# A decoder layer on one Trainium2 core: row maxima scored in pairs of units between whole projection steps

## The chip, the cores and the metric

The kernel runs on one core of one Trainium2 chip. Its engines work side by side, each through its own list of instructions in order: PE (TensorE, the matmuls, with PEld for its weight loads), DVE (VectorE), ACT (ScalarE), POOL (GpSimd) and SP, which issues most of the transfers. They wait for each other by semaphores. Matmuls write to PSUM, which only PE, DVE and ACT reach; the kernel uses it as four tiles. The metric is the device time of one execution in microseconds (us), lower is better.

## The reference

One layer of a decoder in float32, for 4 batches of 512 rows and 512 columns: a causal self attention with 16 heads of 32 columns, a causal cross attention whose keys and values are the context itself (masked scores are -10000, not minus infinity), and a feed-forward part with a gate over 8 experts of which the two highest logits give the weight. Each part takes a layernorm of x and is added to x.

```python
def _layernorm(x, axis=-1, eps=1e-05):
    m = jnp.mean(x, axis=axis, keepdims=True)
    v = jnp.var(x, axis=axis, keepdims=True)
    return (x - m) / jnp.sqrt(v + eps)
...
    def _L0_attn_ref(x, q_w, q_b, k_w, k_b, v_w, v_b, o_w, o_b):
        B, T, H, NH = (4, 512, 512, 16)
        HD = H // NH
        SCALE = HD ** (-0.5)
...
        q = (x @ q_w.T + q_b).reshape(Bd, Td, NH, HD).transpose(0, 2, 1, 3)
        k = (x @ k_w.T + k_b).reshape(Bd, Td, NH, HD).transpose(0, 2, 1, 3)
        v = (x @ v_w.T + v_b).reshape(Bd, Td, NH, HD).transpose(0, 2, 1, 3)
        scores = jnp.einsum('bhqd,bhkd->bhqk', q, k) * SCALE
        causal = jnp.tril(jnp.ones((Td, Td), dtype=bool))
        scores = jnp.where(causal, scores, -jnp.inf)
        probs = jax.nn.softmax(scores, axis=-1)
        ctx = jnp.einsum('bhqk,bhkd->bhqd', probs, v)
        ctx = ctx.transpose(0, 2, 1, 3).reshape(Bd, Td, Hd)
        return ctx @ o_w.T + o_b
...
            scores = jnp.where(causal[None, None], scores, jnp.asarray(MASKED_BIAS, scores.dtype))
            attn = jax.nn.softmax(scores, axis=-1)
            out = jnp.einsum('bhqk,bhkd->bhqd', attn, vh)
...
        logits = jnp.einsum('bsd,ed->bse', x, W_gate)
        routing_weights, selected_experts = jax.lax.top_k(logits, TOP_K)
        shared_out = jnp.einsum('bsd,od->bso', jax.nn.relu(jnp.einsum('bsd,od->bso', x, W_up)), W_down)
        rw = jax.nn.softmax(routing_weights, axis=-1)
        expert_out = jnp.einsum('bsd,do->bso', x, W_expert)
        moe_out = jnp.sum(rw, axis=-1, keepdims=True) * expert_out
        return shared_out + moe_out
    x = x + _L0_attn_ref(_layernorm(x, axis=-1), L0_attn_q_w, ...)
    x = x + _L0_xattn_ref(_layernorm(x, axis=-1), ctx_2048, ctx_2048)
    x = x + _L0_ffn_ref(_layernorm(x, axis=-1), L0_ffn_W_up, ...)
    return x
```

## The kernel before

All work is fp32 in blocks of 128 partitions. x, the queries, keys, values and the intermediate of the feed-forward part of one batch are tiles of 128 x 4 x 512. A *projection step* makes one 128 x 512 block with four accumulating matmuls (`project`, L221, and `project_t`, L233; both are generators that stop after each matmul, so that other work can be put between them). The steps are `query` and `key` (L595, L599), `value` (L642), `up`, `down`, `expert` (L743, L796, L807). `share` and `gate` (L754, L769) are short steps that make the gate's logits; `gate`'s results go through DVE and one ACT exponential into the weights `rw`.

The order on PE, DVE, ACT and POOL is written out by hand: what the Python code issues first stands first in an engine's list. Tiles in PSUM come from one pool of four (`ps`, L63; `pair`, L65, is one tile of 128 x 2 x 512, two banks). A tile's first matmul waits until what was in that place has been read.

The attention needs each row's maximum before the exponentials. `Attention.maxima` (L269) scores one *unit*: heads in four row groups of 32 partitions that work at the same time (L286), into two PSUM tiles; ACT copies each tile to SBUF (L297, in one of six `pt` buffers), POOL masks the diagonal blocks (L305), and DVE takes the maxima (L317). The reductions are not issued at once: `maxima` returns them as a list of *jobs*. A stage has ten units over four groups of heads (g = 0 to 3). When a group's last maxima are there, `split` (L334) cuts them into three bf16 parts, and `rows` (L345) turns these round on PE (L349) and copies them to a row tile `mrow` (L355). `masked` (L359, cross only) broadcasts such a row by a matmul (L363) and takes an exponential (L365); the `weigh` that it returns multiplies the sums `beh` of later keys by it (L371 to L373, on DVE, or on POOL inside the stage).

`with_maxima` (L869) runs such a stage: after each unit it issues a share of the projection matmuls that are to fill PE, in proportion, wherever a step then stands, with one job of the unit before after each matmul. The rows of groups 0 and 1 are turned after units 5 and 7, those of group 2 at the end or, where there is little to fill with, in the attention. `late` tells the attention which rows are still to be made and at which of its units.

`attend` (L917) runs the attention itself in ten units: scores again, with the row maximum added by a bf16 matmul (`scores`, L377: L389, L400), the exponential on ACT (L423), the mask on POOL (L431), and, two units later, the product with the values (`shares`, L450: L462). Denominators come from summed blocks (L510 on DVE, L516 on PE) or from a second matmul with ones. In the cross attention, `divide` (L546: L550, L551 and `inverse`) needs the weighed sums of the group; `scale` (L529) ends a group.

The main loop (L963) runs for each batch b: `with_maxima` and `attend` for the self attention, the output projection, `with_maxima` and `attend` for the cross attention, then `add_cross` (L713: sixteen PE transposes, L718, added to x) and the layernorm and transposes for the feed-forward part (`norm_ffn`, L732). What fills the maxima stages: in batch 0, query, key and value of batch 0 (self) and query and key of batch 1 (cross); in batch 1, the gate, ups and downs of batch 0 (self) and query and key of batch 2 and the experts of batch 0 (cross); in batch 2, the gate, ups and downs of batch 1 (self) and query and key of batch 3 (cross); in batch 3, the experts of batch 1 (self) and the gate, ups and downs of batch 2 (cross). The values of the next batch stand around `add_cross`.

Two neighbouring blocks of a projection share one PSUM tile (`pm_qk`, `pm_v`, `pm_u`, `pm_d`, `pm_e`), and where it can be, one instruction takes both out (L647, L752, L805). `aside` (L823) takes two blocks of downs and two of experts out by ACT and adds them on POOL.

## Time and profile before

| | us |
|---|---|
| median of 3 runs | 811.29 (811.07 to 811.46) |
| the profiled execution, whole | 811.3 |
| the profiled execution, span of the trace | 809.6 |
| PE busy | 796.8 (98%) |
| DVE busy | 563.7 (70%) |
| ACT busy | 397.1 (49%) |
| POOL busy | 334.3 (41%) |

The span is the time from the first to the last instruction in the trace; 1.7 us lie around it. A timeline row gives the start, the time, the engine, the line, the operation with its output and inputs, the shapes, how many instructions were merged (x16), and in brackets how long the engine was idle before and what ended that. A 128x512 fp32 matmul stands in the trace as two rows. Busy times are shares of the whole span: a stage can have another limit.

### The profile page before, as it was taken

To read this page: it belongs to the slowest core of one execution; us is meant where nothing else is said; L and a number is where in the kernel's file an instruction comes from. 1 tells how busy PE (TensorE), PEld (TensorE's weight loads), DVE (VectorE), ACT (ScalarE), POOL (GpSimd) and SP (SyncE) were. 2 spreads that over 40 slices of the span, in tenths; PEclk is the share of its full clock that TensorE was granted. 3 is DMA by queue.
4 is the path that set the end of the run, shared out by engine and by line. 5 is a ranking of instruction groups with operands and counts; after the bars stand their busy time and mean duration, and the time that the engine had idled before them with its cause. 6 is when DMAs were issued, how large, how long until landed. Compare 5 with 4: busy or idle time off the path is not lost.

```text
span 809.6 us, 13953 instructions
## 1 busy us (share of the span) xinstructions
PE 796.8 (98%) x5616; PEld 379.0 (47%) x5616; DVE 563.7 (70%) x955; ACT 397.1 (49%) x450; POOL 334.3 (41%) x525
## 2 busy tenths in 40 slices
PE   8999999999999999999999999999999999999998
PEld 7444454434444454444544445444444344444544
DVE  2478865879678854587867776697879764888512
ACT  2457426861547515666144752686068614674110
POOL 4334612554234732266233481366335543465100
PEclk9999999999999999999999999999999999999999
DMA  9601000001000000020100000000102000000101
GB/s 334 237 28 28 1 1 1 2 2 53 1 27 27 2 1 0 2 101 5 53 14 14 1 2 1 0 2 2 53 28 70 10 1 0 1 2 2 52 1 52
DMA packets 13681, 24.51 MB, mean 30 GB/s; under 512 B 1968, under 2 KB 2224, under 8 KB 13616
## 3 DMA queue, kind: packets, MB, share of 16 engines
q1 hardware_dynamic: 13184, 22.96, 8.3%
q8 instruction: 44, 0.72, 0.4%
q10 hardware_dynamic: 432, 0.66, 0.2%
q14 instruction: 21, 0.17, 0.1%
HBM read 19.42 MB, written 4.19 MB: 29 GB/s over the span
## 4 chain that ended last, share of the span: by engine, by line
PE 86%; DVE 8%; ACT 3%; issue 1%; POOL 1%; DMA 0%
PE pm_qk L235 13%; PE pm_u L235 7%; PE pv_c L462 7%; PE pm_o L687 7%; PE pm_v L223 6%; PE pm_e L223 6%; PE pm_d L223 5%; PE pv_s L462 5%; PE sc_c L389 5%; PE sm_s L286 5%; PE sm_c L286 5%; PE sc_s L389 4%; DVE nm_s L317 3%; DVE nm_c L317 2%; ACT sum_s L423 1%; PE sc_s L400 1%
## 5 line engine op out<-in xcount | busy, mean ns | idle before, releaser
L317 DVE TENSOR_REDUCE nm_c<-s_c 128x2 f32<-128x1024 f32 (+3 forms) x128 | 96.0, 811 | 37.1 <-POOL s_c L305 37.1
L317 DVE TENSOR_REDUCE nm_s<-s_s 128x2 f32<-128x1024 f32 (+3 forms) x128 | 96.9, 811 | 35.2 <-POOL s_s L305 35.2
L297 ACT COPY s_s<-sm_s 128x1024 f32<-128x1024 f32 x80 | 77.1, 1015 | 64.4 <-PE sm_s L286 34.9
L297 ACT COPY s_c<-sm_c 128x1024 f32<-128x1024 f32 x80 | 77.1, 1015 | 39.4 <-PE sm_c L286 23.0
L305 POOL TENSOR_SCALAR_AFFINE_SELECT s_c<-s_c 128x512 f32<-128x512 f32 (+1 forms) x80 | 43.9, 551 | 105.8 <-ACT s_c L297 105.8
L305 POOL TENSOR_SCALAR_AFFINE_SELECT s_s<-s_s 128x512 f32<-128x512 f32 (+1 forms) x80 | 43.8, 551 | 90.7 <-ACT s_s L297 90.7
L423 ACT ACTIVATE pt_c<-sc_c 128x1024 f32<-128x1024 f32 x64 | 61.7, 1031 | 20.5 <-PE sc_c L400 16.2
L510 DVE TENSOR_TENSOR sum_s<-sum_s,pt_s 128x256 f32<-128x256 f32 (+2 forms) x72 | 58.8, 882 | 14.9 <-PE pv_s L462 14.9
L431 POOL TENSOR_SCALAR_AFFINE_SELECT pt_c<-pt_c 128x512 f32<-128x512 f32 (+1 forms) x64 | 51.2, 808 | 26.4 <-ACT pt_c L423 25.9
L223 PE MATMUL pm_d<-wdown_sb,hT 128*128 128x512 f32 x128 | 61.1, 608 | 0.0
L423 ACT ACTIVATE pt_s<-sc_s 128x1024 f32<-128x1024 f32 x56 | 54.1, 1028 | 13.1 <-PE sc_s L400 7.0
L235 PE MATMUL pm_u<-fT,wup_sb 128*128 128x512 f32 x128 | 59.1, 604 | 0.0
L223 PE MATMUL pm_v<-wv_sb,xnT 128*128 128x512 f32 x128 | 58.8, 600 | 0.0
L687 PE MATMUL pm_o<-wo_sb,oT_s 128*128 128x512 f32 x128 | 57.8, 596 | 0.0
L235 PE MATMUL pm_qk<-xnT,wk_sb 128*128 128x512 f32 x120 | 57.3, 607 | 0.0
L223 PE MATMUL pm_e<-wexp_sb,fT 128*128 128x512 f32 x120 | 57.1, 606 | 0.0
L235 PE MATMUL pm_qk<-xnT,wq_sb 128*128 128x512 f32 x120 | 56.7, 604 | 0.0
L389 PE MATMUL sc_s<-qT,kT 32*128 32x128 f32 (+3 forms) x512 | 54.7, 463 | 1.5 <-ACT sum_s L423 1.1
L389 PE MATMUL sc_c<-cqT,ckT 32*128 32x128 f32 (+3 forms) x512 | 54.2, 462 | 0.9 <-ACT sum_c L423 0.9
L431 POOL TENSOR_SCALAR_AFFINE_SELECT pt_s<-pt_s 128x512 f32<-128x512 f32 (+1 forms) x56 | 47.3, 854 | 18.5 <-ACT pt_s L423 18.0
L286 PE MATMUL sm_s<-kT,qT 32*128 32x512 f32 (+3 forms) x512 | 47.5, 461 | 0.1
L286 PE MATMUL sm_c<-ckT,cqT 32*128 32x512 f32 (+3 forms) x512 | 46.1, 460 | 0.0
(166 smaller groups left out, 1274.0 us busy)
## 6 DMA issues: line engine op xcount, KB each, us to landing
cv<-in_ctx_dram SPq DMA_DIRECT2D x16, 256.0 KB, 3.9
out_dram<-x SPq DMA_DIRECT2D x15, 256.0 KB, 2.1
x<-in_x_dram SPq DMA_DIRECT2D x14, 256.0 KB, 4.1
xin<-in_x_dram SPq DMA_DIRECT2D x12, 256.0 KB, 2.6
wq_sb<-in_wq_dram SPq DMA_DIRECT2D x2, 512.0 KB, 6.3
wk_sb<-in_wk_dram SPq DMA_DIRECT2D x2, 512.0 KB, 7.9
wv_sb<-in_wv_dram SPq DMA_DIRECT2D x1, 1024.0 KB, 8.3
wo_sb<-in_wo_dram SPq DMA_DIRECT2D x1, 1024.0 KB, 9.8
```

The costliest lines, as they stand in the source:

```text
L223: nc.tensor.matmul(pm, lhsT=lhs_t[:, c, t * P : (t + 1) * P], rhs=w[:, c, :], start=(c == 0), stop=(c == NC - 1),)
L235: nc.tensor.matmul(pm, lhsT=w[:, c, f * P : (f + 1) * P], rhs=rhs_t[:, c, :], start=(c == 0), stop=(c == NC - 1),)
L286: nc.tensor.matmul(scs[r // 2][:, r % 2, c : c + (i + 1) * P], lhsT=self.q_t[h, g, i * P : (i + 1) * P], rhs=self.k_t[h, g, : (i + 1) * P] ...
L297: nc.scalar.copy(s, scs[n])
L305: nc.gpsimd.affine_select(out=diagonal, in_=diagonal, compare_op=ALU.is_ge, fill=NEG, base=0, pattern=[[0, 2], [0, len(pieces)], [-1, P]], ...
L317: nc.vector.tensor_reduce(self.nm[g][:, i, 2 * n : 2 * n + 2], made[n][:, :, c : c + (i + 1) * P], axis=AX.X, op=ALU.max, negate=True,)
L389: nc.tensor.matmul(scs[r // 2][:, r % 2, c : c + S - j * P], lhsT=self.k_t[h, g, j * P : (j + 1) * P], rhs=self.q_t[h, g, j * P :], start= ...
L423: nc.scalar.activation(pt, scs[n], AF.Exp)
L431: nc.gpsimd.affine_select(out=diagonal, in_=diagonal, compare_op=ALU.is_ge, fill=0.0, base=0, pattern=[[0, 2], [0, len(pieces)], [1, P]], ...
L462: nc.tensor.matmul(pv[r * HD : (r + 1) * HD, u, j * P :], lhsT=ones if u else self.v[:, j, h * HD : (h + 1) * HD], rhs=pts[r // 2][:, r % ...
L510: nc.vector.tensor_tensor(to, to, pts[n][:, :, c : c + S - j * P], ALU.add)
L687: nc.tensor.matmul(pms[t // 2][:, t % 2, :], lhsT=a.out[:, c, t * P : (t + 1) * P], rhs=wo_sb[:, c, :], start=(c == 0), stop=(c == NC - 1),)
```

## The change

A PSUM tile holds one block of a projection, in its first half, and each block is taken out by an instruction of its own: queries and keys at once by ACT, values by DVE, ups by ACT, downs by DVE (the last two of batch 2 by ACT and POOL), experts by DVE with the weight. `aside` is gone.

`with_maxima` scores two units directly after each other (ten units in five rounds) and then runs whole projection steps until half of the next step's matmuls would go beyond the share that is due. Jobs are the second unit's of the round before and the first unit's of this one. In a stage with steps to run beforehand (`first`, only batch 0) one step more is run beforehand. Counting rounds from 0, the rows of groups 0 and 1 are turned after the second matmul of rounds 2 and 3, `masked` comes after the third of rounds 3 and 4; the rows of group 2 are turned at the end only where the last round had two blocks, and otherwise in the attention at unit 3, with those of group 3 at unit 5. Where group 2 was turned in the stage, group 3 comes at unit 3, in the cross attention too. In the cross attention of a stage with a short last round, `masked` of groups 2 and 3 comes at units 6 and 7, and both are weighed at unit 9.

In the feed-forward lists, `gate` follows the first `up` where it followed the last; for batch 2, the first `up` moves from batch 3's cross to its self stage, and `gate` follows the third.

```diff
--- before.py
+++ after.py
@@ -593,23 +593,23 @@
         e.k_t = act.tile([P, NC, S], F32, tag="k_t", name=f"kT_{b}")
 
         def query(f):
-            made[f] = pair(f"pm_qk{b}_{f}")
-            yield from project_t(made[f][:, 0, :], wq_sb, e.xn_t, f)
+            out = pair(f"pm_q{b}_{f}")[:, 0, :]
+            yield from project_t(out, wq_sb, e.xn_t, f)
+            query_out(f, out)
 
         def key(f):
-            yield from project_t(made[f][:, 1, :], wk_sb, e.xn_t, f)
-            out(f)
-
-        def out(f):
+            out = pair(f"pm_k{b}_{f}")[:, 0, :]
+            yield from project_t(out, wk_sb, e.xn_t, f)
+            key_out(f, out)
+
+        def query_out(f, ps):
             nc.scalar.activation(
-                e.k_t[:, f, :], made[f][:, 1, :], AF.Identity, bias=bk_sb[:, f : f + 1]
-            )
+                e.q_t[:, f, :], ps, AF.Identity, bias=bqs_sb[:, f : f + 1], scale=SCALE
+            )
+
+        def key_out(f, ps):
             nc.scalar.activation(
-                e.q_t[:, f, :],
-                made[f][:, 0, :],
-                AF.Identity,
-                bias=bqs_sb[:, f : f + 1],
-                scale=SCALE,
+                e.k_t[:, f, :], ps, AF.Identity, bias=bk_sb[:, f : f + 1]
             )
 
         def half(n):
@@ -628,7 +628,8 @@
                         skip_group_check=True,
                     )
             if n == 1:
-                out(0)
+                key_out(0, made[0][:, 1, :])
+                query_out(0, made[0][:, 0, :])
 
         steps = [(lambda f=f, w=w: w(f)) for f in range(NC) for w in (query, key)]
         if b == 0:
@@ -636,20 +637,13 @@
         return steps
 
     def value(e):
-        b, made = e.b, {}
+        b = e.b
         e.v = act.tile([P, NT, D], F32, tag="v", name=f"v_{b}")
 
         def one(t):
-            if t % 2 == 0:
-                made[0] = pair(f"pm_v{b}_{t}")
-            yield from project(made[0][:, t % 2, :], e.xn_t, wv_sb, t)
-            if t % 2 == 1:
-                nc.vector.tensor_tensor(
-                    e.v[:, t - 1 : t + 1, :],
-                    made[0],
-                    bv_sb.unsqueeze(1).to_broadcast([P, 2, D]),
-                    ALU.add,
-                )
+            made = pair(f"pm_v{b}_{t}")[:, 0, :]
+            yield from project(made, e.xn_t, wv_sb, t)
+            nc.vector.tensor_tensor(e.v[:, t, :], made, bv_sb, ALU.add)
 
         return [(lambda t=t: one(t)) for t in range(NT)]
 
@@ -745,11 +739,9 @@
                 made["h"] = act.tile(
                     [P, NC, S], F32, tag="o_t" if b != B - 2 else "f_t", name=f"hT_{b}"
                 )
-            if f % 2 == 0:
-                made["u"] = pair(f"pm_u{b}_{f}")
-            yield from project_t(made["u"][:, f % 2, :], wup_sb, f_t, f)
-            if f % 2 == 1:
-                nc.scalar.activation(made["h"][:, f - 1 : f + 1, :], made["u"], AF.Relu)
+            u = pair(f"pm_u{b}_{f}")[:, 0, :]
+            yield from project_t(u, wup_sb, f_t, f)
+            nc.scalar.activation(made["h"][:, f, :], u, AF.Relu)
 
         def share():
 
@@ -794,39 +786,24 @@
             nc.vector.tensor_reduce(made["rw"], ew, axis=AX.X, op=ALU.add)
 
         def down(t):
-            if t % 2 == 0:
-                made["d"] = pair(f"pm_d{b}_{t}")
-            yield from project(made["d"][:, t % 2, :], made["h"], wdown_sb, t)
-            if t == NT - 1 and b == B - 2:
-                for n in range(2):
-                    aside(f"d{b}_{n}", t - 1 + n, made["d"][:, n, :], 1.0)
-            elif t % 2 == 1:
-                both = e.x[:, t - 1 : t + 1, :]
-                nc.vector.tensor_tensor(both, made["d"], both, ALU.add)
+            d = pair(f"pm_d{b}_{t}")[:, 0, :]
+            yield from project(d, made["h"], wdown_sb, t)
+            xt = e.x[:, t, :]
+            if t >= NT - 2 and b == B - 2:
+
+                some = work.tile([P, D], F32, tag="xn", name=f"some_{b}_{t}", bufs=4)
+                nc.scalar.copy(some, d)
+                nc.gpsimd.tensor_tensor(xt, xt, some, ALU.add)
+            else:
+                nc.vector.tensor_tensor(xt, d, xt, ALU.add)
 
         def expert(t):
             if b == B - 1 and t == NT - 1:
                 yield from expert_parts(t)
                 return
-            last = b == B - 1 and t == NT - 2
-            if t % 2 == 0:
-                made["e"] = pair(f"pm_e{b}_{t}")
-            yield from project(made["e"][:, t % 2, :], f_t, wexp_sb, t)
-            for n in (0,) if last else (0, 1) if t % 2 == 1 else ():
-                u = t - t % 2 + n
-                if t == NT - 1 and b == B - 3:
-                    aside(f"e{b}_{n}", u, made["e"][:, n, :], made["rw"][:, u : u + 1])
-                    nc.sync.dma_start(out=out[b, u * P : (u + 1) * P, :], in_=e.x[:, u, :])
-                else:
-                    weigh(u, made["e"][:, n, :], slice(0, D), nc.sync)
-
-        def aside(name, t, ps, scale):
-
-
-            some = work.tile([P, D], F32, tag="xn", name=f"some_{name}", bufs=4)
-            nc.scalar.mul(some, ps, scale)
-            xt = e.x[:, t, :]
-            nc.gpsimd.tensor_tensor(xt, xt, some, ALU.add)
+            made_e = pair(f"pm_e{b}_{t}")[:, 0, :]
+            yield from project(made_e, f_t, wexp_sb, t)
+            weigh(t, made_e, slice(0, D), nc.sync)
 
         def weigh(t, ps, cols, queue):
             xt = e.x[:, t, cols]
@@ -870,47 +847,50 @@
 
 
         norms = list(norms)
-        run(steps[:first])
-        fill = matmuls(steps[first:])
-        total = sum(1 if step.__name__ in ("share", "gate") else NC for step in steps[first:])
+
+        run(steps[: first + (first > 0)])
+        steps = steps[first + (first > 0) :]
+
+        def matmuls_of(step):
+            return 1 if step.__name__ in ("share", "gate") else NC
+
+        total = sum(map(matmuls_of, steps))
 
         units = []
         for g in range(0, NC, 2):
             units += [[(g, 1), (g + 1, 1)]]
             units += [u for k in (g, g + 1) for u in ([(k, 2), (k, 0)], [(k, NT - 1)])]
-
-        lead = 2 if first else 0
-        for _ in range(lead):
-            next(fill)
-        done, due, jobs, late = lead, float(lead), [], {5 if a.cross else 3: NC - 1}
-        todo = []
-        for n, pieces in enumerate(units):
-            new = a.maxima(pieces)
-            if todo:
-                todo.pop()(nc.gpsimd)
-            if norms and n % 2 == 0:
-                new.append(norms.pop(0))
-            due += (total - lead) / len(units)
-
-            count = round(due) - done
-            for k in range(count):
-                next(fill, None)
-                done += 1
-                if k == min(1, count - 1) and n in (5, 7):
-                    jobs = a.rows((n - 5) // 2) + jobs
-                if k == min(1, count - 1) and a.cross and n in (6, 8):
-                    todo.append(a.masked((n - 6) // 2))
-                if n == len(units) - 1 and k == count - (2 if count > 4 else 1):
-                    if total >= 2 * len(units):
-                        a.rows(2)[0](nc.scalar.copy)
-                    else:
-                        late = {3: 2, 5: NC - 1}
+        done, jobs, todo = 0, [], []
+        for n in range(0, len(units), 2):
+            jobs += a.maxima(units[n])
+            for weigh in todo:
+                weigh(nc.gpsimd)
+            todo = []
+            new = a.maxima(units[n + 1])
+            if norms:
+                jobs.append(norms.pop(0))
+            part, count = [], 0
+            while steps and done + matmuls_of(steps[0]) / 2 <= total * (n + 2) / len(units):
+                part.append(steps.pop(0))
+                count += matmuls_of(part[-1])
+                done += matmuls_of(part[-1])
+
+            for k, _ in enumerate(matmuls(part)):
+                if k == 1 and n in (4, 6):
+                    jobs = a.rows(n // 2 - 2) + jobs
+                if k == 2 and a.cross and n in (6, 8):
+                    todo.append(a.masked(n // 2 - 3))
                 run(jobs[:1])
                 jobs = jobs[1:]
             run(jobs)
             jobs = new
-        for _ in fill:
-            pass
+        for weigh in todo:
+            weigh(nc.gpsimd)
+        late = {3: NC - 1}
+        if count >= 2 * NC:
+            a.rows(2)[0](nc.scalar.copy)
+        else:
+            late = {3: 2, 5: NC - 1}
         run(jobs)
         return late
 
@@ -939,9 +919,9 @@
             if n in late:
                 for copy in a.rows(late[n]):
                     copy(nc.scalar.copy)
-            if a.cross and n in (5, 7):
-                todo.append(a.masked(n // 2))
-            if n in (6, 9) and todo:
+            if a.cross and n in ((5, 7) if len(late) == 1 else (6, 7)):
+                todo.append(a.masked(2 + n // 7))
+            while todo and (n == 9 or n == 6 and len(late) == 1):
                 todo.pop(0)()
             if len(waiting) > 2:
                 values()
@@ -999,13 +979,14 @@
                 pass
             gates, ups, downs, experts = ffn(e)
             if b + 3 < B:
-                between_self, between_cross = gates[:1] + ups + gates[1:] + downs, experts
+                between_self = gates[:1] + ups[:1] + gates[1:] + ups[1:] + downs
+                between_cross = experts
             elif b + 2 < B:
-                between_self, between_cross = gates[:1] + ups + gates[1:] + downs, []
-                ahead = experts
+                between_self = gates[:1] + ups[:1] + gates[1:] + ups[1:] + downs
+                between_cross, ahead = [], experts
             elif more:
-                between_self, ahead = ahead, experts
-                between_cross = gates[:1] + ups + gates[1:] + downs
+                between_self, ahead = ahead + ups[:1], experts
+                between_cross = gates[:1] + ups[1:3] + gates[1:] + ups[3:] + downs
             else:
                 run(gates[:1] + ups + gates[1:])
                 run(downs[:2] + experts[:2] + downs[2:] + experts[2:])
```

## The prediction

> **What bounds the kernel now.** I read the page's busy times first, then the chain of waits, then the timeline of single stages, engine by engine.
>
> ```profile
> PE 796.8 (98%) x5616; PEld 379.0 (47%) x5616; DVE 563.7 (70%) x955; ACT 397.1 (49%) x450; POOL 334.3 (41%) x525
> ...
> PE 86%; DVE 8%; ACT 3%; issue 1%; POOL 1%; DMA 0%
> ```
>
> The tensor engine (PE) is almost never without work, at a granted clock of 1.00 in every stretch I read, and 86% of the chain that ends last is its own. So what counts is how long PE needs for its list, and each wait that the change puts into that list. The change is made in the eight maxima stages (two for each batch: self and cross). This is the timeline of the cross stage of batch 0:
>
> ```profile
> 129.06 1.15 PE L286 MATMUL sm_c<-ckT,cqT 32*128 32x384 f32 x16
> 130.14 1.98 PE L235 MATMUL pm_qk<-xnT,wk_sb 128*128 128x512 f32 x4
> 130.30 1.93 ACT L297 COPY s_c<-sm_c 128x1024 f32<-128x1024 f32 x2 [1.07 <-PE sm_c L286]
> ...
> 132.06 1.14 PE L286 MATMUL sm_c<-ckT,cqT 32*128 32x512 f32 x8
> 132.16 0.69 ACT L604 ACTIVATE kT<-pm_qk,bk_sb 128x512 f32<-128x512 f32 x1
> ...
> 133.13 1.98 PE L235 MATMUL pm_qk<-xnT,wq_sb 128*128 128x512 f32 x4
> ```
>
> A unit starts every 2.99 us (129.06, 132.06, then 135.04). Two rows of the trace are one projection matmul; eight rows in a run take 3.43 us, so one takes 0.859 and two 1.72. A unit's own streaming is 0.86 (in the attention after it, sixteen such rows from 251.95 to 252.81, with row-tiled work on both sides). What is left, 2.99 - 1.72 - 0.86 = 0.41, is what going from full-array to row-tiled matmuls and back costs. The copies out of PSUM start 1.24 after the unit (130.30 - 129.06), and two take 1.93.
>
> **Part 1: two units together.** Each of 5 pairs in 8 stages saves one such round trip: 40 x 0.41 = 16.4 us. But PSUM has four tiles, a pair takes all four, and the order of the changed program shows every first projection after a pair waiting for the copy of the first unit's first tile. The attention loop has the same situation: a third unit meets four occupied tiles.
>
> ```profile
> 252.15 1.94 ACT L423 ACTIVATE sum_s<-sc_s 128x1024 f32<-128x1024 f32 x2 [0.69 <-PE sc_s L400]
> ...
> 253.23 0.30 PEld L389 LDWEIGHTS sc_s<-qT,kT 32*128 32x128 f32 x4 [0.22 <-ACT sum_s L423]
> ```
>
> The first exponential of 0.97 to 1.02 ends near 253.15, PE goes on 0.08 later. So after a pair: copy starts at 1.24, ends at 2.24, PE is released at 2.32, and with some 0.1 for a full weight load the projection starts 2.40 after the pair, where without the wait it would be 1.07 + 0.86 = 1.93. A pair then costs 2.40 + 0.19 (back to row-tiled: 1.91 for two matmuls of 1.72) = 2.59, against 2 x (2.99 - 1.72) = 2.54 now. The saving is used up: +0.05 x 40 = **+2.0 us**. Ends: released at 2.26 with nothing added, 40 x -0.09 = -3.6; started at 2.55, 40 x 0.20 = +8.
>
> The Trainium skill, TensorEngine Tiling (Array Packing), Key Properties, says that changing the tiling mode drains the engine, which speaks for the change; by that alone the time would be the 811.3 less the 16.4 above, 795. The same page under PSUM Bottleneck speaks against it: tiling makes the matmuls faster but not the evacuation, which can become the limit; no price is given there, and the rows above decide.
>
> **Part 2: one block to a PSUM tile.** Evacuations get shorter and more: adds of 128x1024 at 1.22 become two of 0.68, relus of 1.02 two of 0.69. ACT's extra 8 x 0.36 lies in its idle time (24 of 31 us busy in the busiest stage for its length); that cover gone, it would be 3 us. VectorE (DVE) is in order, and here it matters where it stands at a stage's end. Now, in batch 1's self stage (attention starts at 250.77):
>
> ```profile
> 248.13 1.27 DVE L317 TENSOR_REDUCE nm_s<-s_s 128x2 f32<-128x768 f32 x2
> 250.65 1.22 DVE L805 TENSOR_TENSOR x<-pm_d,x 128x1024 f32<-128x1024 f32 x1 [1.25 <-PE pm_d L223]
> 251.79 1.27 DVE L317 TENSOR_REDUCE nm_s<-s_s 128x2 f32<-128x768 f32 x2
> 252.98 0.54 DVE L206 TENSOR_SCALAR xn_a<-xin,mv_a,rs_a 128x512 f32<-128x512 f32 x1
> 253.43 2.34 DVE L317 TENSOR_REDUCE nm_s<-s_s 128x2 f32<-128x1024 f32 x2
> ```
>
> DVE is waiting for PE there, it is not late. In the changed order it is tied to PE by the add of down block 1, which ends with the round before the last. From the last round's start T it then has, from T + 0.2: add 0.66, two reduces 1.23, four 2.46, a norm 1.25, two reduces 2.35, the split 0.9, add (block 2) 0.66, four reduces 2.46, add (block 3) 0.66: done at T + 12.8. (Durations from this stage's rows; single adds from L702, 678 ns.) The second score unit of the attention takes over block 3's PSUM tile. PE gets there at T + 2.40 + 8 x 0.859 + 0.33 (transposes) + 0.1 + 1.18 (first unit, 250.77 to 251.95) = T + 10.9. A wait of 1.9, and the same in batch 2: **+3.8** (ends 0 and 6). Behind the blocked matmul stand all scores, and ACT's exponentials with them.
>
> **Part 3: whole steps, so DVE's tie to a block's end comes in every round.** Where DVE evacuates single blocks (values in batch 0's self stage, experts in batch 3's self stage, downs in batch 3's cross stage), the second pair's transposes (L349) come early. Tied at a round's start R: add 0.66 to 0.75, reduces 1.27 and 2.35, split 0.9 (cross 1.2), so the parts are there at R + 5.3 to 5.6; PE asks at R + 2.40 + 1.72 = R + 4.1. Waits of 1.2, 1.3 and 1.4; with 0.3, 0.2 and 0.6 for the lesser ones (a late add, the first transposes) **+1.5, +1.5, +2.0** (ends 0 and 8 together). In the stages between, where ACT evacuates, DVE isn't tied and I find nothing.
>
> **Part 4: an up step moved from batch 3's cross to its self stage.** 4 x 0.859 is paid in both places, 0 in sum. In the self attention there PE now waits 1.43 and 0.27 because DVE is late; with 3.4 us more cover that goes: **-1.7** (ends -1.7, 0). The gate's steps cost PE the same 0.92 wherever they stand; only its tile comes free sooner.
>
> **Part 5: cross transposes and weighing moved.** Where the last round has one block (cross of batches 0, 2, 3), rows of group 2 go into the attention, and the weighing of group 2 goes from unit 6 to unit 9, in front of group 3's on DVE:
>
> ```profile
> 173.64 0.06 DVE L371 MEMSET ct_c<- 128x1 f32 x1 [1.37 <-ACT ct_c L365]
> 173.73 1.06 DVE L372 TENSOR_TENSOR behT<-ct_c,behT 128x512 f32<-128x512 f32 x1
> 174.83 0.69 DVE L373 TENSOR_TENSOR ct_c<-ct_c,cnt 128x512 f32<-128x512 f32 x1
> ...
> 185.61 0.06 DVE L371 MEMSET ct_c<- 128x1 f32 x1
> ...
> 188.17 0.69 DVE L550 TENSOR_TENSOR ct_c<-pv_c,ct_c 128x512 f32<-128x512 f32 x1 [0.43 <-PE pv_c L516]
> ...
> 193.97 0.69 DVE L532 TENSOR_TENSOR behT<-behT,dt_c 128x512 f32<-128x512 f32 x1
> ```
>
> At 173.64 the weighing is between two waits, free. After the other at 185.61 there is only 0.43 of slack, so 1.9 of weighing makes everything behind it 1.5 late, up to L532. The last four of the sixteen L718 transposes (PE from 193.30, twelve take 1.3) read that result: no slack. 3 x 1.5, and 0.2 each for the value evacuation now in front of the layernorm transposes: **+5.1** (ends 0, 6). Against it, unit 5 now has the L363 matmul right behind the transposes, and PE waits 2.3 us there over all (the L363 group's idle time, released by ACT); taken apart, **-2.3** (ends -2.3, 0).
>
> **Sum.** 2.0 + 3.8 + 1.5 + 1.5 + 2.0 - 1.7 + 5.1 - 2.3 = +11.9 on the span of 809.6, so 821.5; the profiled execution's 811.3 has 1.7 around the span, which gives 823.2, and the median of the runs (811.29) is the same as the profiled one. Forecast: **823 us**. No DMA is added or moved to another queue; POOL's adds for two expert blocks become DVE's (in part 3).
>
> **Rivals.** (a) Heavy: DVE's ties bite in every round, not only at these places. Then the pair's last score tile waits for a DVE add that stands behind a reduce of 1.21: 0.7 more in each of the 16 or so rounds that end with such a block, +11, to 834. For it: 563.7 us of in-order DVE work; against: ACT evacuates the other rounds, and the add's own end (0.15 + 0.66) lies just before the need at 0.95. (b) Wash: the copy's wait eats the switches, but DVE runs far enough ahead at the stages' ends and the tails have slack that I don't see: 809.6 + 2.0 - 1.7 - 2.3 + some 2 of ties, 811 to 812. Against it stands the missing slack at 193.97. (c) Faster, decided by one thing, the time from a pair's start to its first projection: if it is 2.26 instead of 2.40, pairs give -3.6, and if DVE's delays also stay hidden, the freed waits of 1.7 and 2.3 come on top: 804. It turns faster when that time is below 2.35 and the other terms are near nothing. Against it: the copy alone ends at 2.24. That the edit doesn't do what it says is excluded by the order of the instructions.
>
> **How the numbers follow.** Forecast 0.62, (a) 0.15, (b) 0.11, (c) 0.12. The forecast's own range is 816 to 830. Leaving out most of (c) and half of (a), the range is 809 to 833; the sum of all lower ends would be 804, of all upper ends 839. A difference under 0.2% (1.6 us) can't be told from none. Faster: (c) and a little of (b), 0.13; same: half of (b), 0.05; slower 0.82.
>
> **What would show it.** In a maxima stage, projections should start 2.3 to 2.5 after the first L286 of a pair, with waits on L297's copy; if 1.93, part 1 is wrong by 19 us. Around the start of batch 1's and 2's self attention, a PE wait of about 2 on the down add; in three stages a wait before L349; at the end of three cross attentions, a wait of 1.5 inside the transposes of add_cross. DVE waiting for PE at those places instead would make the forecast wrong, toward 811.

## The result, and the profile after

The changed kernel takes 820.92 us (median of 4 runs, 820.8 to 821.1) beside 811.37 (4 runs, 811.07 to 811.46) for the kernel before, measured with it: ratio 1.0119, 95% interval 1.0106 to 1.0131. It is slower by 9.5. The profiled spans are 819.1 and 809.6.

The page of the kernel after, its busy times and its chain of waits by engine:

```profile
PE 785.8 (96%) x5616; PEld 380.3 (46%) x5616; DVE 565.0 (69%) x972; ACT 398.2 (49%) x456; POOL 327.7 (40%) x523
...
PE 39%; DVE 11%; ACT 3%; issue 2%; DVEq 0%; ACTq 0%
```

PE is busy 11.0 less than before: switches were saved. The span is 9.5 longer all the same, so PE now waits some 20 us more. The chain of waits could here be followed back only to 368 us, over 55% of the span; of these 55%, VectorE has 11, a fifth, where before it had 8 of 99. The same stage as in the prediction, batch 0's cross stage, in the timeline of after:

```profile
133.76 2.01 PE L286 MATMUL sm_c<-ckT,cqT 32*128 32x512 f32 x24
134.99 3.76 ACT L297 COPY s_c<-sm_c 128x1024 f32<-128x1024 f32 x4 [0.43 <-PE sm_c L286]
136.05 3.70 PE L235 MATMUL pm_q<-xnT,wq_sb 128*128 128x512 f32 x8 [0.29 <-ACT s_c L297]
```

The pair starts at 133.76, the first of four copies at 134.99, and the projection at 136.05, 0.29 late, released by the copy. The waits that the prediction placed on VectorE (DVE), in self stage 0, cross stage 3, self attention 1 and at the end of cross attention 0:

```profile
55.42 0.38 PE L349 MATMUL mt_s<-identb,parts 128*128 128x128 bf16 x4 [1.06 <-ACT s_s L297]
...
710.96 0.40 PE L349 MATMUL mt_c<-identb,parts 128*128 128x128 bf16 x4 [1.29 <-DVE parts L343]
...
256.06 1.15 PE L389 MATMUL sc_s<-qT,kT 32*128 32x128 f32 x16 [1.62 <-DVE x L798]
...
197.91 0.66 PE L712 MATMUL tp_x<-ident,behT 128*128 128x128 f32 x4 [0.90 <-DVE behT L532]
```

All four places wait. (The first row names ACT, whose copy was long done; the transposes read what DVE's split writes.) In before, the sixteen transposes of the last place ran through without a wait:

```profile
193.30 2.08 PE L718 MATMUL tp_x<-ident,behT 128*128 128x128 f32 x16
```

By the starts of the first score matmuls of each stage and attention, this is where the time went, after less before:

| | stage | attention | from there to the next stage |
|---|---|---|---|
| self 0, with the lead in | +0.39 | +1.36 | 0.00 |
| cross 0 | +0.20 | +0.29 | +1.00 |
| self 1 | -0.98 | +1.21 | 0.00 |
| cross 1 | +0.32 | -0.07 | +0.06 |
| self 2 | -0.98 | +1.20 | 0.00 |
| cross 2 | +0.21 | +0.29 | +0.95 |
| self 3, less the moved step's 3.43 | +1.34 | -2.09 | 0.00 |
| cross 3, with it; last column to the last expert block | +2.55 | +0.78 | +1.12 |

The maxima stages, where the switches are saved, gain 2.0 in two places and lose 5.0 in the others, +3.05 in sum. The attentions add 2.97 and what stands between them and the next stage 3.13; 0.3 more lies behind the last row.

### The profile page after: what moved, and what is told of

It reads as the page before. It is cut to its first block, busy times and chain, and to the rows that moved or that the text cites. A ratio compares the mean times of both kernels' runs of the same rounds, so it can differ in the third digit from the quotient of the medians.

```text
span 819.1 us, 13977 instructions
## 1 busy us (share of the span) xinstructions
PE 785.8 (96%) x5616; PEld 380.3 (46%) x5616; DVE 565.0 (69%) x972; ACT 398.2 (49%) x456; POOL 327.7 (40%) x523
## 4 chain that ended last, share of the span: by engine, by line
PE 39%; DVE 11%; ACT 3%; issue 2%; DVEq 0%; ACTq 0%
PE pm_u L235 5%; PE pm_e L223 4%; PE pm_o L681 3%; PE pm_d L223 3%; PE pm_v L223 3%; PE pv_c L462 3%; DVE nm_c L317 3%; PE pv_s L462 3%; PE sc_s L389 2%; DVE nm_s L317 2%; PE sc_c L389 2%; PE pm_k L235 2%; PE pm_q L235 2%; PE sm_s L286 1%; PE sm_c L286 1%
## 5 line engine op out<-in xcount | busy, mean ns | idle before, releaser
L317 DVE TENSOR_REDUCE nm_s<-s_s 128x2 f32<-128x1024 f32 (+3 forms) x128 | 96.6, 809 | 29.8 <-POOL s_s L305 29.8
L317 DVE TENSOR_REDUCE nm_c<-s_c 128x2 f32<-128x1024 f32 (+3 forms) x128 | 95.7, 809 | 29.4 <-POOL s_c L305 29.4
L223 PE MATMUL pm_d<-wdown_sb,hT 128*128 128x512 f32 x128 | 59.0, 601 | 2.3 <-ACT s_c L297 1.1
L431 POOL TENSOR_SCALAR_AFFINE_SELECT pt_c<-pt_c 128x512 f32<-128x512 f32 (+1 forms) x64 | 49.2, 777 | 27.1 <-ACT pt_c L423 26.5
L235 PE MATMUL pm_k<-xnT,wk_sb 128*128 128x512 f32 x120 | 56.0, 602 | 1.9 <-ACT s_c L297 1.7
L235 PE MATMUL pm_q<-xnT,wq_sb 128*128 128x512 f32 x120 | 55.2, 597 | 1.4 <-ACT s_c L297 1.1
L223 PE MATMUL pm_e<-wexp_sb,fT 128*128 128x512 f32 x120 | 55.2, 600 | 1.3 <-ACT s_s L297 0.7
L389 PE MATMUL sc_c<-cqT,ckT 32*128 32x384 f32 (+3 forms) x512 | 54.6, 461 | 1.4 <-ACT sum_c L423 0.9
L257 ACT COPY fT<-tp_f 128x1024 f32<-128x1024 f32 x8 | 8.0, 1013 | 79.6 <-PE tp_f L251 79.6
L286 PE MATMUL sm_c<-ckT,cqT 32*128 32x512 f32 (+3 forms) x512 | 42.2, 448 | 0.4 <-ACT s_c L297 0.2
```

Source lines behind the costliest of these rows:

```text
L223: nc.tensor.matmul(pm, lhsT=lhs_t[:, c, t * P : (t + 1) * P], rhs=w[:, c, :], start=(c == 0), stop=(c == NC - 1),)
L235: nc.tensor.matmul(pm, lhsT=w[:, c, f * P : (f + 1) * P], rhs=rhs_t[:, c, :], start=(c == 0), stop=(c == NC - 1),)
L286: nc.tensor.matmul(scs[r // 2][:, r % 2, c : c + (i + 1) * P], lhsT=self.q_t[h, g, i * P : (i + 1) * P], rhs=self.k_t[h, g, : (i + 1) * P] ...
L317: nc.vector.tensor_reduce(self.nm[g][:, i, 2 * n : 2 * n + 2], made[n][:, :, c : c + (i + 1) * P], axis=AX.X, op=ALU.max, negate=True,)
L389: nc.tensor.matmul(scs[r // 2][:, r % 2, c : c + S - j * P], lhsT=self.k_t[h, g, j * P : (j + 1) * P], rhs=self.q_t[h, g, j * P :], start= ...
L431: nc.gpsimd.affine_select(out=diagonal, in_=diagonal, compare_op=ALU.is_ge, fill=0.0, base=0, pattern=[[0, 2], [0, len(pieces)], [1, P]], ...
```

## The experiments

Two numbers are used: the median with its ratio to the kernel before (1.0119 for after), and stage lengths of the profiled executions, which repeat to 0.02 where nothing changed. Only the time up to the first scores, with the loading of the inputs, differs by up to 0.6 among profiles of the same start, and the very end by 0.3. In some executions the granted clock falls once for a few us, which costs 1.1 to 1.7 (shown in the last section); where that is in a number it is said.

**Does the copy's end set the start of the projection?** Two runs, a control for the PSUM tiles and one in which the copy is made in halves.

```diff
 def pair(name):
-    return ps.tile([P, 2, S], F32, tag="ps", name=name)
+    if not ring:
+        return ps.tile([P, 2, S], F32, tag="ps", name=name)
+    ring.append(ring.pop(0))
+    return ring[-1]
...
+        if a.name != "c3":
+            ring.extend([pair(f"ring_{a.name}_{n}") for n in range(4)])
...
```

> The kernel after, with only the bookkeeping of its PSUM tiles changed: in seven of the eight maxima stages (not in batch 3's cross stage) the four tiles are taken once at the start of the stage and used in turn, so that a wait is for the part of a tile that is really still being read, not for the whole tile. Every instruction is the same. This is the control for the next run. Theory: the turn is the same and the first projection still waits for the copy of a whole tile: 820.9 +-1. Rival: waits for whole tiles (a block's second half, which nobody uses) cost something: 818 or less.

Measured: 823.64 (823.19 to 824.05), ratio 1.0147 (1.0131 to 1.0162); the fall of the clock is in all four runs. Without it the spans differ by +1.5: +0.66 in cross stages 0 and 2, presumably because the tiles come round in another order there, and +0.23 ahead of the first scores, within what that time varies by. The rival is out, and the control counts for the next run, in which the copy of the first tile of each pair's first unit is made in halves:

```diff
-                nc.scalar.copy(s, scs[n])
+                if halves and n == 0:
+                    nc.scalar.copy(s[:, 0, :], scs[n][:, 0, :])
+                    nc.scalar.copy(s[:, 1, :], scs[n][:, 1, :])
+                else:
+                    nc.scalar.copy(s, scs[n])
...
```

> As the control, and in those seven stages ACT copies the first tile of each pair's first unit in two halves of 128x512, so that the first projection after the pair waits for the first half only. Theory of the prediction's part 1 (the switch is saved, 0.41 a unit, and the wait for the copy gives it back): with a half copy of 0.6 instead of 1.02 the projection starts 1.93 instead of 2.29 after the pair's start, 0.36 less in some 33 rounds, -12 at the most and, as DVE's ties take a part, -5 to -12: 809 to 816. Rival 1: DVE's ties to block ends decide the rounds, the wait for the copy only moves: 0 to -2. Rival 2: the two halves make ACT late (some 0.2 more each): +2.

Measured: 824.65 (823.8 to 825.59), ratio 1.0161 (1.0148 to 1.0175), slower than its control (two of the four runs have the fall of the clock; the profiled spans without it are 820.6 for the control and 822.1 for this run) where 5 to 12 less were expected. The timeline of this run shows why:

```profile
134.27 2.01 PE L291 MATMUL ring_c<-ckT,cqT 32*128 32x512 f32 x24
135.50 0.59 ACT L303 COPY s_c<-ring_c 128x512 f32<-128x512 f32 x1 [0.43 <-PE ring_c L291]
135.98 0.59 ACT L304 COPY s_c<-ring_c 128x512 f32<-128x512 f32 x1
136.62 3.70 PE L240 MATMUL ring_c<-xnT,wq_sb 128*128 128x512 f32 x8 [0.35 <-ACT s_c L304]
```

The first half is done at 136.09, but PE starts at 136.62, 0.05 after the second. In the kept trace ACT gives no signal at the end of the first half, only one at 136.58, and it signals as often (457 times) as in the control, which has fewer copies: both halves are signalled with the second one. So a wait for half a tile was not tried. What the run does show is the other direction: the copy ends 0.06 later, the projection starts 2.35 instead of 2.29 after its pair, and self stages 1 and 2, of five rounds each, become 0.30 longer than the control's. The copy's end passes into the time one to one.

**Is the pairing worth anything?**

```diff
-            new = a.maxima(units[n + 1])
...
+            turn = NC if count >= 2 * NC else 2
             for k, _ in enumerate(matmuls(part)):
+                if k == turn - 1:
+                    new = a.maxima(units[n + 1])
```

> The kernel after with the units taken apart again, all else kept (whole steps, a tile for each block, the order of steps, the late rows): in a round of two steps unit, step, unit, step; in a round of one step unit, two matmuls, unit, two matmuls. The theory, with the sizes that the profile after shows: a pair costs 2.48 and two single units 2.54, so -0.06 x 40 is lost again, +2.4, 823; DVE's ties stay. Rival 1: pairing itself does the harm (the wait for the copy of 0.28 in 40 places, and DVE fed in lumps): -3 or more, 818 or less. Rival 2: the saved switches come through in full: +16, 837.

Measured: 822.69 (822.64 to 823.13), ratio 1.0143 (1.0129 to 1.0157), near the theory's 823, but all four runs have the fall of the clock, the profiled one in self stage 0. Without its some 1.5 the run is 0.3 longer than after. By stages: cross 0 and 2, one step to a round, -0.1; self 1 and 2 +0.45; cross 1 +1.16; self 0 some +1.6, where one wait for DVE's parts grew to 2.27; against it cross 3 -1.5 and self 3 and the attentions of self 1 and 2 -0.4 each. So pairs bring next to nothing, and they are not what does the harm.

**The waits on DVE, one by one.** First the transposes (part 3), then the order at a stage's end (part 2).

```diff
-                if k == 1 and n in (4, 6):
+                if k == (1, 3)[n == 6] and n in (4, 6):
```

> The kernel after, with the transposes of group 1's maxima two matmuls (1.7 us) later in their round, in all eight stages. Theory of part 3: DVE, tied to a block's end, has the parts ready 0.4 to 1.3 after PE asks, in four of the stages (0.42, 0.88 and 1.29, 0.64 and 1.12, 1.06 in the profile after); the waits for group 1 (0.42, 1.29, 1.12, 1.06) go: -2 to -4, 817 to 819. Rival: the tie is to DVE's whole amount of work, so the wait comes back at the next thing that DVE hands over: 0.

Measured: 818.22 (817.22 to 818.44), ratio 1.008 (1.0068 to 1.0093), -2.7: as expected in sum. The stages gain 0.55 to 0.65 in five places and 1.47 in cross 3, self attentions 1 and 2 0.5 each, but three cross attentions give 1.1 each back: there the product with group 0's sums (L516) now starts before DVE has them all, and takes 2.09 instead of 1.22 in cross attention 0. That is the rival, at three of eight places. DVE's split of group 3 stands in front of these sums, which the next run changes:

```diff
+        a.tail = [jobs.pop()] if a.cross and len(late) == 2 else []
         run(jobs)
         return late
...
+            if n == 3:
+                run(a.tail)
```

> As the run with group 1's transposes two matmuls later (818.22), and in the three late cross attentions the split of group 3's maxima is issued behind the sums of group 0 on DVE. In that run the five maxima stages without late rows kept their gain, but each late cross attention gave 1.1 back at the product with group 0's sums. Theory: DVE's order is what gives it back (1.9 of split in front of the sums), so about 1.1 x 3 comes off: 815. Rival: DVE's whole work is the bound there, and the wait moves to the transposes of group 3: 818.

Measured: 815.72 (815.32 to 817.52), ratio 1.0054 (1.004 to 1.0067): -5.2 against after, near the theory's 815. Of the 1.1 that cross attentions 0 and 2 gave back, 0.24 is left, now a wait of the late transposes of group 3.

```diff
+        adds_last = not a.cross and a.name in ("s1", "s2")
...
-                run(jobs[:1])
-                jobs = jobs[1:]
+                if n < 8 or k < 3 or not adds_last:
+                    run(jobs[:1])
+                    jobs = jobs[1:]
             run(jobs)
```

> The kernel after, where in the last round of batch 1's and 2's self stage the maxima that stand on DVE between the last two down adds are issued behind the last add. Same work, another order on DVE. Theory of part 2: the second score unit of the attention, which waits 1.62 for the add of down block 3, no longer waits: -1.2 to -1.6 in each of the two attentions, -2.4 to -3.2, 818. Rival: DVE is late by its whole work, so the wait comes back as one on the row parts or on the sums inside the same attention: 0.

Measured: 819.06 (818.34 to 820.04), ratio 1.0098 (1.0084 to 1.0112); two of the four runs have the fall of the clock. The two attentions become 1.15 and 1.14 shorter, nothing else moves by more than 0.07: -2.3, just short of the theory. In this run's timeline the second score unit of self attention 1 follows without a wait:

```profile
254.06 0.44 PE L400 MATMUL sc_s<-mrow_s,onesb 32*128 32x512 bf16 x4
254.27 1.09 PE L389 MATMUL sc_s<-qT,kT 32*128 32x128 f32 x16
```

**The weighing of group 2 (part 5).** Two places for it:

```diff
-            while todo and (n == 9 or n == 6 and len(late) == 1):
+            while todo and n in ((6, 9) if len(late) == 1 else (7, 9)):
```

> The kernel after, with the weighing of group 2 of the three late cross attentions (batches 0, 2 and 3) issued one unit after its mask matmul (unit 7) instead of at unit 9 in front of group 3's. Theory of part 5: DVE's tail then ends about 1 earlier, as the wait of 0.90 before the last transposes of the cross attention shows: -0.9 x 3 = -2.7, 818.2. Rival: the weighing at unit 7 stands in front of the additions that the value products wait for, and gives the same back there: 0.

Measured: 823.07 (822.7 to 825.33), ratio 1.0148 (1.0133 to 1.0162), +2.1. The tails gain 0.96 to 0.99 each, as expected, but each attention loses 1.6 before it: the rival, and more than it said. In this run's timeline of cross attention 0 PE waits for the sums, here and inside the group:

```profile
189.82 1.67 PE L516 MATMUL pv_c<-sum_c,ones 128*32 128x512 f32 x6 [0.39 <-DVE sum_c L510]
```

In after DVE is idle for 4.21 ahead of group 1's division, so the next run puts the weighing there, with the mask matmul that it needs two units earlier:

```profile
179.34 0.69 DVE L550 TENSOR_TENSOR ct_c<-pv_c,ct_c 128x512 f32<-128x512 f32 x1 [4.21 <-PE pv_c L462]
```

```diff
-            if a.cross and n in ((5, 7) if len(late) == 1 else (6, 7)):
+            if a.cross and n in ((5, 7) if len(late) == 1 else (4, 7)):
...
-            while todo and (n == 9 or n == 6 and len(late) == 1):
+            while todo and n in ((6, 9) if len(late) == 1 else (5, 9)):
```

> The kernel after, where in the three late cross attentions the mask matmul of group 2 is issued at unit 4 instead of 6 and its weighing at unit 5 instead of 9, so that the weighing falls into DVE's idle 4.21 before the second division. The run with the weighing at unit 7 took the wait of 0.90 at the tail away (0.96 less from the transposes on in each) and lost 1.62 earlier in each attention, where the product with the sums came to wait for DVE. Theory: the price of part 5 is only where the 1.9 of weighing stands; in the gap it costs nothing, and the tail's 0.96 x 3 comes off: -2.9, 818.0. Rival: any earlier weighing makes DVE late for the sums: +1 or more.

Measured: 818.56 (818.5 to 818.62), ratio 1.0091 (1.0077 to 1.0105), -2.4. The tails gain 0.93 to 0.97 each and the attentions lose 0.17, 0.18 and 0.33. The same 1.9 of DVE's work costs 1, 1.6 or 0.2 by where it stands.

**The change taken apart from the other side.** The kernel before with one block to a tile (part 2's edit alone), and that with the changed order of steps (part 4):

```diff
-            made[f] = pair(f"pm_qk{b}_{f}")
-            yield from project_t(made[f][:, 0, :], wq_sb, e.xn_t, f)
+            out = pair(f"pm_q{b}_{f}")[:, 0, :]
+            yield from project_t(out, wq_sb, e.xn_t, f)
+            query_out(f, out)
...
```

> The kernel before with one part of the change alone: every projected block gets a PSUM tile and an evacuation of its own (part 2). Units stay single, the matmuls stay spread in proportion, the order of steps and the late rows are those of before. Theory: DVE's lateness at the stage's end came with whole steps and the held-back block; alone the shorter and more numerous evacuations cost next to nothing: 811.3 to 812.5. Rival 1: the extra evacuations themselves make DVE late, as in the forecast's 1.9 at two attentions: 814 to 815. Rival 2: tiles come free sooner: 809 to 810.

Measured: 811.92 (11 runs, 811.77 to 812.92) beside 811.15, ratio 1.0012 (1.0003 to 1.0021), +0.8: theory. Neither self attention 1 nor 2 changes (0.00), so DVE's lateness there isn't due to the shorter evacuations. The +0.8 is a balance, though: cross stage 3 is 1.9 longer than before, 1.3 of it at this place, where PE waits for the add of a single down block:

```profile
702.85 1.13 PE L286 MATMUL sm_c<-ckT,cqT 32*128 32x512 f32 x4 [0.23 <-DVE x L798]
```

All the rest together is about 1.4 shorter (without the fall of the clock in this profile). So single blocks alone already tie PE to DVE at this place.

```diff
-                between_self, ahead = ahead, experts
-                between_cross = gates[:1] + ups + gates[1:] + downs
+                between_self, ahead = ahead + ups[:1], experts
+                between_cross = gates[:1] + ups[1:3] + gates[1:] + ups[3:] + downs
...
```

> As the run with single blocks alone, and the changed order of steps (part 4): one up step of batch 2 moves from batch 3's cross stage to its self stage, and gate's step comes two steps earlier in four stages. Theory: the move takes away the self attention's waits of 1.43 and 0.27 and costs nothing elsewhere: -1.7 against the run with single blocks. Rival: the cross stage loses that cover and waits for DVE as much as was won: 0.

Measured: 807.57 (807.44 to 807.77), ratio 0.9956 (0.9942 to 0.997): -4.35 against single blocks alone, over twice the theory, and faster than both kernels. On its page PE is busy 99% and DVE's share of the chain is 5%:

```profile
PE 793.7 (99%) x5616; PEld 375.3 (47%) x5616; DVE 565.0 (70%) x972; ACT 399.4 (50%) x456; POOL 331.3 (41%) x523
...
PE 90%; DVE 5%; ACT 2%; issue 1%; DMA 0%
```

The wait that the theory wanted to take away stands in before's self attention 3:

```profile
630.27 2.09 PE L516 MATMUL pv_s<-sum_s,ones 128*32 128x512 f32 x8 [1.43 <-DVE sum_s L510]
```

It is gone here, but it was gone already with single blocks alone, in whose self stage 3 PE waits 1.03 for an expert block's addition instead. What the new order adds is elsewhere: beyond the moved step's own 3.43, cross stage 3 gains 1.7, about what single blocks alone had cost there.

What separates this kernel from after is only how `with_maxima` and `attend` lay out the rounds: pairs, whole steps, late rows and late weighing. That is worth 820.92 - 807.57 = 13.35 by the medians, 13.1 with each beside its own measurement of before (811.37 and 811.15), and 13.3 by the profiled spans.

**All reorderings together, and one more step from the fast one.**

```diff
-                if k == 1 and n in (4, 6):
+                if k == 3 and n in (4, 6):
...
+        late = {3 if a.cross else 5: NC - 1}
...
+        if not a.cross:
+            jobs, a.tail = jobs[:-3], jobs[-3:]
+        elif len(late) == 2:
+            a.tail = [jobs.pop()] + [lambda w=w: w(nc.gpsimd) for w in todo]
...
```

> The kernel after with all the reorderings together: transposes of groups 0 and 1 two matmuls later; in the three late cross attentions group 2 masked at unit 4 and weighed at unit 5, group 3's split and group 1's weighing (POOL) behind group 0's sums; in the self stages the last unit's maxima and split behind group 0's sums; in batch 1's and 2's self stage the maxima of the last round behind the last add. No work is added or taken away. Theory: the ties of in-order engines are what the change lost, so the sum of the single gains (-5.4, -2.2, -2.3, from the runs so far) and of the new ones (-1.5 for group 0's transposes, about -1.2 for batch 0's self attention, -0.8 for POOL in batch 3's cross attention) comes off: 807 to 808, below both kernels. Rival: DVE's whole work binds, and each reordering moves the wait: 811 or more.

Measured: 820.45 (820.1 to 820.64), ratio 1.0114 (1.01 to 1.0128), a miss by 13; the fall of the clock is in every run. The stages keep their gains and the tails theirs, but the self attentions are 0.9 to 1.3 longer than after's and the late cross attentions 1.1 to 1.5. The timeline has new waits of PE, here in self attention 1 and cross attention 0:

```profile
265.43 1.61 PE L389 MATMUL sc_s<-qT,kT 32*128 32x512 f32 x6 [1.22 <-ACT pt_s L423]
...
174.08 0.40 PE L349 MATMUL mt_c<-identb,parts 128*128 128x128 bf16 x4 [1.47 <-DVE behT L551]
```

Both go back to work that was moved. In self attention 1 the exponential waits 2.86 itself, for the held-back maxima (L317), whose input lies in one of the six `pt` buffers that the exponentials also write to. In cross attention 0 the division (L550) follows on DVE directly behind group 3's split, which was moved ahead of it. The split's first instruction takes 1.26, beside POOL's weighing, which was moved there too; in the run with only the split moved it takes 0.16.

```profile
264.35 1.94 ACT L423 ACTIVATE pt_s<-sc_s 128x1024 f32<-128x1024 f32 x2 [2.86 <-DVE nm_s L317]
...
169.93 1.26 DVE L338 TENSOR_TENSOR nm_c<-nm_c,nfloor 128x16 f32<-128x16 f32 x1
...
172.74 0.69 DVE L550 TENSOR_TENSOR ct_c<-pv_c,ct_c 128x512 f32<-128x512 f32 x1
```

So at these two places the moved work made something else wait, as the rival said. That is read from the timeline and the code; no run takes these moves back one by one.

```diff
-            if a.cross and n in (5, 7):
-                todo.append(a.masked(n // 2))
+            if a.cross and n in (4, 7):
+                todo.append(a.masked(2 + n // 7))
```

> As the run with single blocks and the changed order of steps (807.57), and in the four cross attentions the mask matmul of group 2 at unit 4 instead of 5; its weighing stays at unit 6. In that run PE waits 0.58 to 0.60 in front of this matmul in each cross attention, for an exponential that frees its PSUM tile (the term of -2.3 in the forecast's part 5). Theory: two units earlier in ACT's list there is a free tile, the waits go: -0.6 x 4 = -2.3, 805.3, the fastest so far. Rival: a tile is short there too, and the wait moves to the next scores: 807.6.

Measured: 806.74 (806.7 to 807.21), ratio 0.9946 (0.9932 to 0.9959), the fastest. In cross attention 0 the wait that the run without this edit has (first row) is gone from the mask product, but one stands behind it, at the value products, half as long:

```profile
171.17 0.38 PE L363 MATMUL mb_c<-mrow_c,same 128*128 128x512 bf16 x1 [0.58 <-ACT sum_c L423]
...
166.96 0.39 PE L363 MATMUL mb_c<-mrow_c,same 128*128 128x512 bf16 x1
...
168.18 0.64 PE L462 MATMUL pv_c<-pt_c,cv 128*32 128x256 f32 x8 [0.26 <-ACT pt_c L423]
```

So 0.16 in three attentions and 0.32 in the fourth are won, 0.8 of 2.3: between theory and rival.

## Why the prediction was right, and where it was not

The direction, the forecast case (823 for 820.92) and nearly all places of the waits are right. The parts that make up the rounds and their order were put at 2.0 + 3.8 + 5.0 + 5.1 - 2.3 = 13.6; the runs say 13.35. Part 2's edit and part 4 alone were put at -1.7; they are +0.8 - 4.35 = -3.6. Several sizes are off and offset each other; that the sums agree so closely is partly luck. By places, the forecast had +7.0 in the stages (2.0 + 5.0), -0.2 in the attentions (3.8 - 1.7 - 2.3) and +5.1 behind them; the table above has +3.05, +2.97 and +3.13.

- **Part 1, mechanism right, size wrong.** The forecast had the projection 2.40 after the pair's start; it is 2.29 (2.24 to 2.30 in 39 of the 40 pairs). The failing step is the 0.1 added for a weight load, a term that no row had shown: the copy starts at 1.23 and takes 1.0, and the start follows its end by 0.06, with the weight load's row beginning in the same instant as the matmul's. From one pair to the next it is 5.92 (133.76 to 139.68), less the step's four matmuls, 3.44, so a pair costs 2.48 instead of 2.59, and 40 of them -2.4 instead of +2.0. The forecast's own turning point for "faster" was 2.35, so rival (c)'s condition was met; it failed on its second half, that the DVE terms be near nothing. Taking the pairs apart cost 0.3, not 2.4, so even this gain was not there in the sum. The price of a pair alone wasn't measured: in that run waits on DVE changed as well, by 1.5 in cross stage 3 for example.
- **Part 2, mechanism right, size too large.** The wait was put at 1.9 and is 1.62; the attentions lose 1.2 each and the reordering gives 1.15 back. That is +2.4 instead of +3.8.
- **Part 3, right by the waits, partly in place.** Waits of 1.2, 1.3 and 1.4 were forecast for the second transposes; 1.06, 1.12 and 1.29 are there, and with the lesser ones of 0.64 and 0.88 they make 5.0, as forecast. "In the stages between DVE isn't tied and I find nothing" was wrong: cross 0, 1 and 2 wait 0.42. The two repairs gave 5.2, but only half of it in the three stages of the forecast (0.55, 0.61 and 1.48). Not forecast was that DVE's next hand-over binds right behind: the first repair alone got only half.
- **Part 4, sign right, too small.** Self attention 3 gains 2.09 (forecast 1.7), and the wait of 1.43 that the forecast named is gone in after. Between single-block kernels the new order of steps is worth 4.35, of which gate's place gives 0.25 in each of two stages; "0 in sum" for the two stages was the failing step: there cross stage 3 gains 1.7, self stage 3 1.4 (less 1.1 for a fall of the clock in the run it is compared with) and self attention 3 0.7. The first of these takes back what single blocks alone had cost in that stage.
- **Part 5, too large.** The wait at the tails was put at 1.5 and is 0.90; with the layernorm's part the tails lose 1.00, 0.95 and 1.12. That is +3.1 instead of +5.1. The mask waits, put at -2.3, are gone in after, but no cross attention is shorter by more than 0.07; where they were taken away alone it brought 0.8, with a new wait of 0.26 for an exponential at the next product.
- **Not forecast:** self attention 0's +1.36. One more set of transposes stands in it (0.32), the product with the sums takes 1.65 instead of 1.04, and a wait of 0.27 for an exponential stands behind it. The rest wasn't settled, and the one reordering tried for it made it longer. Of cross attention 3's +0.78, most is a wait of 0.91 for POOL's mask at the first value products, which was 0.26 before.
- **Rivals.** (a) would have DVE bind at every round's end; it binds in the places named. (b) needed DVE far ahead; the four waits shown are against it.

## What to carry to other kernels

A saved switch on a busy engine is worth only what the buffers allow: when two units fill all of PSUM, the next matmul starts at the end of the first copy (0.06 behind it here), and of the 16.4 of saved switches at most 2.4 are left before anything else is looked at. In this kernel the work that two in-order engines exchange is better given in small pieces spread in proportion: bunching it into pairs and whole steps, with the late rows and weighing that came with it, left the amount of DVE's work as it was (565.0 busy in both) and cost 13, much of it through where that work stood. The same 1.9 on DVE cost 1, 1.6 or 0.2 by its place, and six repairs that gained alone or were expected to gain didn't add up, so look for the idle gap in the engine's own timeline and measure the sum.

## What the runs showed of the hardware

**PE's granted clock halves for a while in some executions.** In the run with the units apart, PE waits 2.27 in self stage 0, and the step behind it takes 3.25 instead of the 1.94 that four such rows take after the transposes of cross stage 3 in after. The second fence is the table by windows for that stretch; its columns are the stretch and its length, the busy time of PE, PEld, DVE, ACT and POOL with the number of their instructions, the granted clock, and the share and rate of the DMA:

```profile
55.47 0.38 PE L349 MATMUL mt_s<-identb,parts 128*128 128x128 bf16 x4 [2.27 <-DVE parts L343]
55.69 3.25 PE L223 MATMUL pm_v<-wv_sb,xnT 128*128 128x512 f32 x4
```

```profile
55.60:59.00 3.40, 3.40 (x12) 1.14 (x10) 2.44 (x7) 0.00 (x0) 2.17 (x4) 0.58 0.24 80
```

The granted clock is 0.58 over 3.40, which is a loss of some 1.4 in this window; the fall itself is 0.50 over 56.17 to 59.58. Five more profiled runs show such a fall, and it costs 1.1 to 1.7 each time. With single blocks alone a wait of 1.03 stands ahead of it. In the other four, such as the run with the split behind the sums, where it comes at 685, no wait over 0.20 stands ahead of it in that stage, so what sets it off is open here. The Trainium skill, TensorE: Matmul & The Clock Gate, What's actually happening, says that the clock halves after an idle window of about 3.4 us. Half speed for 3.4 would be 1.7, which agrees with the size; no run here shows an idle stretch of that length before it (the longest is the 2.27), so the measurement doesn't bear out that condition.

**DVE waits for POOL.** The same instruction in two splits in after, that of group 2 at the end of cross stage 0 and that of group 3, which DVE reaches only inside the attention, and what POOL does during the first:

```profile
158.22 1.29 POOL L373 TENSOR_TENSOR ct_c<-ct_c,cnt 128x512 f32<-128x512 f32 x1
158.44 1.10 DVE L341 TENSOR_TENSOR rest_c<-nm_c,parts 128x16 f32<-128x16 f32 x1
165.89 0.18 DVE L341 TENSOR_TENSOR rest_c<-nm_c,parts 128x16 f32<-128x16 f32 x1
```

The first takes 1.10 and ends 0.03 after POOL's product of two operands, the second, with no such product on POOL, takes 0.18. The Trainium skill, SBUF — State Buffer, SBUF: two separate sides, says that the two engines take turns at a shared pair of ports, the one that started first for its whole instruction; the three rows agree. So 0.9 of DVE's lateness at this place is POOL's weighing, which the prediction didn't count for DVE.
